# Linear attention of one layer: a list schedule in place of a hand-written round order, PSUM banks divided by use, its own weights loaded first

## The chip, the cores and the metric

The kernel runs on one core of a Trainium2 chip. The core has five engines that run side by side and wait for one another through semaphores: PE (TensorE, the matmuls; PEld is its weight load), DVE (VectorE), ACT (ScalarE), POOL (GpSimd) and SP (SyncE, which here only issues DMAs). Each engine executes its own instructions strictly in the order in which they stand in its queue. SBUF is the working memory of 128 partitions. PSUM, which the matmuls write, has eight banks of 2 KB a partition; a tile of 128 x 512 float32 fills one.

The metric is the device time of one execution in microseconds (us). The kernel before took 3962.16 us, the median of three runs (3951.46, 3962.16, 3969.95).

## The reference

The program is four layers of a network over x of shape 4 x 32 x 128 x 128 (batch, t, n, feature), all float32: graph attention with a state-space scan, a Fourier-domain attention, **linear attention and a mixture of experts (layer 2)**, a second softmax attention and a recurrent layer. The change is within the first half of layer 2, cut here to what it computes (`bs` 4, `seq` 4096, 8 heads of 16):

```python
def _ln_t(v, eps=1e-5):
    m = jnp.mean(v, axis=-1, keepdims=True)
    s = jnp.var(v, axis=-1, keepdims=True)
    return (v - m) / jnp.sqrt(s + eps)

def _L2_attn_ref(Q, Wq, bq, Wk, bk, Wv, bv, Wo, bo):
    q = (Q @ Wq + bq).reshape(bs, seq, N_HEADS, HEAD_DIM)
    k = (Q @ Wk + bk).reshape(bs, seq, N_HEADS, HEAD_DIM)
    v = (Q @ Wv + bv).reshape(bs, seq, N_HEADS, HEAD_DIM)
    phi_q = jax.nn.elu(q) + 1.0
    phi_k = jax.nn.elu(k) + 1.0
    KV = jnp.einsum('blhd,blhm->bhdm', phi_k, v)
    K_sum = phi_k.sum(axis=1)
    Z = 1.0 / (jnp.einsum('blhd,bhd->blh', phi_q, K_sum) + EPS)
    V_new = jnp.einsum('blhd,bhdm->blhm', phi_q, KV) * Z[..., None]
    return V_new.reshape(bs, seq, N_HEADS * HEAD_DIM) @ Wo + bo

t = t + _L2_attn_ref(_ln_t(t), ...)          # layer 2, first half
t = t + _L2_ffn_ref(_ln_t(t), ...)           # layer 2, experts
```

All keys of a batch element must be summed into KV before its first query can be answered.

## The kernel before

The activations stay in SBUF for the whole program, in the tile X: 128 images of 128 x 128, 32 for each batch element. Layer 2's attention (`linear_attention`, L2001) works on groups of four images, 128 x 512 numbers; there are 32 groups u, eight for each batch element. Each group passes two halves.

The **first half** makes the keys. *stats* (DVE, L2033, L2035, and L250 for the added epsilon) and *power* (POOL, L251, one over the root) give the layer norm's factors. *norm* (DVE, L2042, four instructions) writes xn. *turn* (PE, L257, four transposes into a PSUM bank "pt") and a copy by ACT (L2051, called *turned* below) give ln, the transposed group, which is kept in one of 12 buffers until its queries. *keys* (PE, L2056) multiplies ln by Wk and Wv side by side into the two banks "pk". *keys_out* is four instructions: ACT copies the values (L2063, *vout*), DVE adds the key bias (L2064, *kadd*), ACT makes a relu and an exponential (L2066, L2067, *krelu* and *kexp*). *keys_elu* (DVE, L2071, *kelu*) finishes phi(k), and *gather* (PE, L2078) adds the group to KV in the bank "pKV". After eight groups *gathered* (DVE, L2088 to L2091) takes KV out.

The **second half** answers the queries: *queries* (PE, L2095, into a bank "pt"), *queries_out* (ACT, L2100, L2101, L2102: two relus that read the bank, and an exponential; *qout* and *qexp* below), *queries_elu* (POOL, L2105, *qelu*), *attend* (PE, L2111, into the two banks "pn"), *attended* (DVE, L2117 to L2119), *back* (PE, L257, transposes into "pt") with a copy by ACT (L2129, *backed*), *project* (PE, L2135, into "pt"), and *add* (DVE, L2141), which adds the result to X. *bias* (POOL, L2138) adds bo to X and may run any time after the group's norm.

The order on each engine is written out by hand. A loop of 46 rounds (L2150) calls every step once, each for a group that lies a fixed number of rounds back; queries come ten rounds after stats. `in_order` ties each engine's instructions to just that order:

```python
            for r in range(U + 14):
                do(norm, r - 1)
                do(keys, r - 2)
                do(queries, r - 10)
                ...
                do(project, r - 13)
                do(stats, r)
                do(add, r - 13)
                ...
```

PSUM is divided so: three banks "pt", which turn, queries, back and project take in turn; two "pk"; two "pn"; one "pKV". `layer2` (L2175) first asks SP for the first eight loads of the experts' weights, 1 MB each (`expert_load`, L2194), and then calls `layer2a`, whose first lines ask SP for the attention's own nine small weights (L200 and L2008). The route, the experts and the scatter of layer 2 follow it.

Other stages of the same program, the graph attention of layer 0 (L384 on) and the attention of layer 3 (L2563), already use a planner, `Parts` (L124). A stage adds its parts to it, each with its engine, an assumed cost in us, the parts that it comes after, the buffers that it takes and frees ("holds" with a limit), and a rank. `emit` (L166) then builds the program part by part: among the first `window` parts left it looks for those whose inputs and buffers are settled, finds the earliest possible start by the assumed costs, and among the parts of that engine that could start within `patience` of it takes the one of lowest rank. So the order on each engine is fixed when the program is built; at run time the engines follow it and wait where a semaphore is late.

Of the kernel before, what the change touches and what calls it, by code (L numbers as in the profile page):

```python
# [19 lines left out]
P = 128  # L20
# [167 lines left out]
class Kernel:  # L188
# [1807 lines left out]
    def layer2a(self):  # L1996
        with self.pool("l2c", 1) as c, self.pool("l2w", 2) as w:
            with self.pool("l2pt", 3, True) as pt, self.pool("l2pk", 1, True) as pk, self.pool("l2pv", 1, True) as pv:
                self.linear_attention(c, w, pt, pk, pv)

    def linear_attention(self, c, w, pt, pk, pv):  # L2001
# [10 lines left out]
        vs = [c.tile([P, 4, P + 1], F32, tag=f"v{i}", name=f"v{i}") for i in range(2)]  # L2012
# [6 lines left out]
        def bank():  # L2019
            return pt.tile([P, 4, P], F32, tag="pt", name="pt")  # L2020
# [7 lines left out]
        def stats(u):  # L2028
            st = w.tile([P, 4, 6], F32, tag="st", name="st")
            mv = S[u]["mv"] = w.tile([P, 4, 2], F32, tag="mv", name="mv")  # L2030
            rs = S[u]["rs"] = w.tile([P, 4], F32, tag="rs", name="rs")
            for i in range(4):
                nc.vector.bn_stats(st[:, i, :], xs(u)[:, i, :])  # L2033
            for i in range(4):
                nc.vector.bn_aggr(mv[:, i, :], st[:, i, :])  # L2035
            self.rsqrt(rs, mv[:, :, 1], 1e-5)
# [9 lines left out]
        def turn(u):  # L2046
            p = bank()
            x = S[u].pop("xn")
            self.transposes(p, [x[:, i, :] for i in range(4)])
            S[u]["ln"] = w.tile([P, 512], F32, tag="ln", name="ln", bufs=12)  # L2050
            nc.scalar.copy(S[u]["ln"], flat(p))  # L2051
# [6 lines left out]
        def keys_out(u):  # L2058

            p = S[u].pop("kv")  # L2060
            k = S[u]["k"] = w.tile([P, 4, P], F32, tag="k", name="k")
            m = S[u]["m"] = w.tile([P, 4, P], F32, tag="m", name="m")
            nc.scalar.copy(vs[u % 2][:, :, :P], p[:, :, 1, :])  # L2063
            nc.vector.tensor_tensor(k, p[:, :, 0, :], bk.unsqueeze(1).to_broadcast([P, 4, P]), ALU.add)  # L2064

            nc.scalar.activation(m, k, AF.Relu, scale=-1.0)  # L2066
            nc.scalar.activation(m, m, AF.Exp, scale=-1.0)  # L2067
# [5 lines left out]
        def gather(u):  # L2073
            if u % 8 == 0:
                KV["p"] = pv.tile([P, P + 1], F32, tag="pKV", name="pKV")
            k = S[u].pop("k")
            for i in range(4):
                nc.tensor.matmul(  # L2078
                    KV["p"], k[:, i, :], vs[u % 2][:, i, :], start=(u % 8 == 0 and i == 0), stop=(u % 8 == 7 and i == 3)
                )  # L2080

        def gathered(u):

            if u % 8 == 7:
                p = KV.pop("p")
                t = KV[u // 8] = w.tile([P, P + 8], F32, tag="KV", name="KV")
                ks = w.tile([P, 1], F32, tag="ks", name="ks")
                nc.vector.tensor_copy(ks, p[:, P : P + 1])  # L2088
                nc.vector.scalar_tensor_tensor(t[:, :P], bv, ks, p[:, :P], ALU.mult, ALU.add)
                nc.vector.tensor_tensor(t[:, :P], t[:, :P], m16, ALU.mult)  # L2090
                nc.vector.tensor_scalar(t[:, P:], m16[:, 0:P:16], ks, None, ALU.mult)  # L2091

        def queries(u):
            S[u]["pq"] = bank()
            nc.tensor.matmul(flat(S[u]["pq"]), Wq, S[u].pop("ln"), start=True, stop=True)  # L2095

        def queries_out(u):
            q = S[u]["q"] = w.tile([P, 512], F32, tag="q", name="q")
            m = S[u]["m"] = w.tile([P, 512], F32, tag="mq", name="mq")
            nc.scalar.activation(m, flat(S[u]["pq"]), AF.Relu, scale=-1.0, bias=nbq)  # L2100
            nc.scalar.activation(q, flat(S[u].pop("pq")), AF.Relu, bias=bq)  # L2101
            nc.scalar.activation(m, m, AF.Exp, scale=-1.0)  # L2102

        def queries_elu(u):
            nc.gpsimd.tensor_tensor(S[u]["q"], S[u]["q"], S[u].pop("m"), ALU.add)  # L2105
# [18 lines left out]
        def back(u):  # L2124
            p = bank()
            z = S[u].pop("z").rearrange("p a h d -> p a (h d)")
            self.transposes(p, [z[:, i, :] for i in range(4)])
            S[u]["zT"] = w.tile([P, 4, P], F32, tag="zT", name="zT")
            nc.scalar.copy(S[u]["zT"], p)  # L2129

        def project(u):
            p = S[u]["po"] = bank()
# [10 lines left out]
        def do(f, u):  # L2143
            if 0 <= u < U:
                f(u)

        nbq = c.tile([P, 1], F32, tag="nbq", name="nbq")
        nc.vector.tensor_scalar(nbq, bq, -1.0, None, ALU.mult)
# [866 lines left out]
```

## Time and profile before

| what | value |
|---|---|
| three runs | 3951.46, 3962.16, 3969.95 us |
| profiled execution, its own time | 3967.12 us |
| span of the profiled execution | 3965.3 us |
| mean granted PE clock | 0.888 of full speed |
| busy PE / DVE / ACT / POOL over the span | 81% / 78% / 66% / 61% |
| linear attention: first stats (L2033) to end of last add (L2141) | 2959.0 to 3252.6 us |
| first keys (L2056); keys of group 2; keys of group 9 | 2975.6; 2990.8; 3030.1 us |
| last gather (L2078) | 3221.1 us |

The profile is of one execution; it is some 5 us slower than the median of the three runs. A row of a timeline or a group gives the start or the sum, the duration, the engine, the line, the operation, the tiles out<-in, the shapes and the count; in square brackets or behind the bar stands the idle time of the engine just before, and what ended it. DVE's 78% over the whole program says little of one stage; this case is read from the 294 us of the linear attention.

### The profile page before, as it was taken

What the parts mean: (1) busy time and instruction counts of PE and PEld (TensorE: products, weight loads), DVE (VectorE), ACT (ScalarE), POOL (GpSimd) and SP (SyncE); (2) the same over time, 40 slices, a digit from 0 to 9 for tenths busy, and PEclk for the clock granted to TensorE, in tenths of its full rate; (3) what the DMA queues carried; (4) which work ended last, traced back from release to release, by engine and by line L of the source; (5) the groups of instructions that cost most, each with busy time, mean ns of one, the idle gap of its engine ahead of it and who ended that gap; (6) DMA issues with size and microseconds to landing.
All of it is one profiled execution on the core that took longest, in us unless ns stands there. A gap on an engine that the chain in (4) does not pass through costs nothing. (4 is left out here: it accounts for less than half of the span.)

```text
span 3965.3 us, 64167 instructions
## 1 busy us (share of the span) xinstructions
PE 3227.2 (81%) x23297; PEld 2075.9 (52%) x23297; DVE 3090.5 (78%) x7595; ACT 2609.6 (66%) x5093; POOL 2400.4 (61%) x1786
## 2 busy tenths in 40 slices
PE   6888887888888888878888869787847787988877
PEld 3445544444544454544444548655535663587655
DVE  6799997799997799997899975668757866286952
ACT  5799875798864798865899853334544556166763
POOL 2599883699873699973799860233444443066940
PEclk8999889999888999998999885888769998998999
DMA  3000000000000000000000000000020000600003
GB/s 122 1 1 1 1 1 1 1 1 1 1 1 1 1 1 1 1 1 1 1 1 1 1 17 2 1 1 1 1 87 8 1 1 1 256 7 1 1 1 86
DMA packets 51548, 61.34 MB, mean 15 GB/s; under 512 B 5743, under 2 KB 31036, under 8 KB 51100
## 3 DMA queue, kind: packets, MB, share of 16 engines
q1 hardware_dynamic: 36636, 42.12, 3.1%
q10 hardware_dynamic: 14592, 15.08, 1.1%
q8 instruction: 187, 3.06, 0.3%
q14 instruction: 133, 1.09, 0.1%
HBM read 48.79 MB, written 8.39 MB: 14 GB/s over the span
## 5 line engine op out<-in xcount | busy, mean ns | idle before, releaser
L667 POOL TENSOR_TENSOR e<-dt,Ar 128x1024 f32<-128x1024 f32 x496 | 1160.9, 2362 | 103.4 <-ACT pa L673 101.0
L695 DVE SCALAR_TENSOR_TENSOR S<-u,BC,pa 128x256 f32<-128x256 f32 x1984 | 820.8, 476 | 28.4 <-PE yp L710 0.5
L687 DVE TENSOR_TENSOR pa<-pa,S 128x1024 f32<-128x1024 f32 x496 | 607.3, 1224 | 49.3 <-ACT pa L673 49.0
L673 ACT ACTIVATE pa<-e 128x1024 f32<-128x1024 f32 x496 | 504.8, 1023 | 126.8 <-DVE S L695 114.4
L710 PE MATMUL yp<-S,D 64*64 64x256 f32 x4096 | 378.4, 414 | 101.7 <-DVE S L695 87.3
L710 PE MATMUL yp<-S,Dp 64*64 64x256 f32 x4096 | 342.9, 452 | 51.2 <-DVE S L695 38.4
L710 PEld LDWEIGHTS yp<-S,D 64*64 64x64 f32 x4096 | 186.4, 140 | 264.4 <-DVE S L695 153.8
L465 POOL TENSOR_TENSOR e<-e,den 128x512 f32<-128x512 f32 x128 | 132.2, 1043 | 257.2 <-DVE den L461 193.2
L710 PEld LDWEIGHTS yp<-S,Dp 64*64 64x64 f32 x4096 | 175.7, 153 | 203.5 <-issue 118.1
L679 ACT ACTIVATE D<-I,BC 128x64 f32<-128x64 f32 x1024 | 260.7, 334 | 0.6 <-PE yp L710 0.6
L889 PE MATMUL pm<-h,Wm 128*128 128x512 f32 x512 | 240.1, 604 | 1.2 <-ACT h L525 1.2
L728 PE MATMUL pm<-I,y 128*128 128x64 f32 x1024 | 165.1, 289 | 89.7 <-ACT y L718 89.7
L453 ACT ACTIVATE e<-sc,mn 128x128 f32<-128x128 f32 x512 | 143.9, 391 | 98.1 <-DVE mn L448 96.6
L728 PEld LDWEIGHTS pm<-I,y 128*128 128x128 f32 x1024 | 152.4, 214 | 101.9 <-ACT y L718 101.9
L673 ACT ACT_TABLE_LOAD x144 | 184.8, 1283 | 19.4 <-DVE S L695 17.2
L684 POOL TENSOR_TENSOR Dp<-I,BC 128x256 f32<-128x256 f32 x256 | 164.4, 660 | 20.1 <-PE yp L710 10.4
L251 POOL TENSOR_TENSOR rs<-rs,mhalf 128x4 f32<-128x4 f32 (+1 forms) x33 | 38.6, 1171 | 220.0 <-DVE rs L250 181.7
L448 DVE TENSOR_REDUCE mn<-sc 128x4 f32<-128x512 f32 x128 | 83.4, 685 | 87.8 <-PE sc L440 55.9
L889 PEld LDWEIGHTS pm<-h,Wm 128*128 128x128 f32 x512 | 90.9, 191 | 92.3 <-issue 90.2
L723 PE MATMUL pm<-xc,DD 128*128 128x128 f32 x512 | 127.8, 334 | 5.3 <-ACT sz L859 4.6
L723 PEld LDWEIGHTS pm<-xc,DD 128*128 128x128 f32 x512 | 87.6, 210 | 64.9 <-issue 38.0
L2607 ACT ACTIVATE xn<-X,xnb,xrs 128x128 f32<-128x128 f32 x192 | 80.7, 488 | 42.6 <-DMA lnw<-in_L_attn_ln_w_dram 30.3
(587 smaller groups left out, 8025.7 us busy)
## 6 DMA issues: line engine op xcount, KB each, us to landing
w<-in_L_ffn_weight_dram SPq DMA_DIRECT2D x22, 1024.0 KB
w<-in_L_ffn_weight_dram ACTq DMA_DIRECT2D x10, 1024.0 KB
out_dram<-o ACTq DMA_DIRECT2D x16, 256.0 KB
out_dram<-o SPq DMA_DIRECT2D x16, 256.0 KB
X<-in_x_dram SPq DMA_DIRECT2D x4, 512.0 KB
A<-in_L_conv_A_log_dram SPq DMA_DIRECT2D x1, 2048.0 KB
cw<-in_L_conv_conv_w_dram SPq DMA_DIRECT2D x1, 512.0 KB
sh<-in_sh_dram SPq DMA_DIRECT2D x1, 512.0 KB
```

The lines of the kernel that those rows point to most:

```text
L453: nc.scalar.activation(e[:, i, :], v["sc"][:, h, i * P : (i + 1) * P], AF.Exp, scale=-1.0, bias=v["mn"][:, 4 * h + i : 4 * h + i + 1],)
L465: nc.gpsimd.tensor_tensor(v["e", h], v["e", h], den, ALU.mult)
L667: nc.gpsimd.tensor_tensor(v["e", q], node("dt").unsqueeze(1).to_broadcast([P, 4, 256]), Ar[:, 4 * q : 4 * q + 4, :], ALU.mult)
L673: nc.scalar.activation(v["a", q], v.pop(("e", q)), AF.Exp, scale=-1.0)
L679: nc.scalar.activation(v["D", q][:, r, :], I2, AF.Copy, scale=g["BC"][:, i, s : s + 1])
L684: nc.gpsimd.tensor_tensor(v["D", q], I2.unsqueeze(1).to_broadcast([P, 4, 64]), C, ALU.mult)
L687: nc.vector.tensor_tensor(v["a", q], v["a", q], S[:, 4 * q : 4 * q + 4, :], ALU.mult)
L695: nc.vector.scalar_tensor_tensor(S[:, s, :], node("u"), Bt, a[:, r, :], ALU.mult, ALU.add)
L710: nc.tensor.matmul(v["y"][o : o + 64, n, :256], D[ns, r, :], S[ns, s, :], start=(s < 2), stop=(s >= 14), skip_group_check=True,)
L723: nc.tensor.matmul(v["p"][:, j * P : (j + 1) * P], DD[:, j, :], g["xc"][:, j, cs], start=True, stop=False)
L728: nc.tensor.matmul(v["p"][:, o : o + 64], v["y"][:, n, j * P : (j + 1) * P], I2, start=False, stop=(n == 1))
L889: nc.tensor.matmul(g["x", j], Wm[:, i, j * P : (j + 1) * P], rows(4 * k + 3 - i), start=(i == 0), stop=(i == 3))
```

## The change

The loop of rounds is gone. Every step becomes one or more parts of a planner (`window` 300, `patience` 0.3), all 32 groups in one plan, and the order on each engine is what the planner makes of it. For that, steps are cut finer: the rsqrt into a DVE part and a POOL part (power), turn and back into a PE part and an ACT copy (turned, backed), keys_out into vout, kadd, krelu and kexp, queries_out into qout and qexp. The second half of group u enters the plan behind the first half of group u + 8; the ranks are `at` x 125.5 plus a number by kind.

The PSUM banks are divided by use: "pt" has two banks, for turn and back; a new bank "pq" is for queries and project; "pk", "pn" and "pKV" stay as they were. stats' small tiles have three buffers in place of two, and there are three value tiles v in place of two (one more memset of its column of ones). Instructions and shapes are otherwise the same.

The eight expert loads are asked for after the attention's own nine loads, by the `loads()` that `layer2` passes in.

In the order that the planner makes, nbq stands first on DVE, then stats0, stats1, norm0, norm1, stats2, stats3, kadd0; PE begins turn0, keys0, turn1, queries0, keys1, turn2, turn3, gather0, keys2. From the middle of the plan PE reads "keys21 back10 queries12 attend11 turn22 gather20 back11 keys22 project9 attend12 queries13 turn23 back12 project10 keys23 attend13 queries14 gather21 back13 project11 turn24 queries15 keys24 project12 attend14 queries16 gather22 back14 project13 attend15 queries17 turn25 back15 project14 keys25"; DVE "kadd21 stats26 kelu21 attended11 norm24 stats27 kadd22 add9 attended12 kelu22 norm25 stats28 add10 attended13 kadd23 add11 kelu23 norm26 stats29 add12 attended14 kadd24 add13 kelu24 attended15"; POOL takes bias some two groups after its norm. After gather31 eight attends, six queries and ten projects are left.

```diff
-    def layer2a(self):
+    def layer2a(self, loads):
         with self.pool("l2c", 1) as c, self.pool("l2w", 2) as w:
-            with self.pool("l2pt", 3, True) as pt, self.pool("l2pk", 1, True) as pk, self.pool("l2pv", 1, True) as pv:
-                self.linear_attention(c, w, pt, pk, pv)
+            with self.pool("l2pt", 2, True) as pt, self.pool("l2pk", 1, True) as pk:
+                self.linear_attention(c, w, pt, pk, loads)
...
+    L2_RANKS = dict(
+        add=432.5, attend=163, attended=143.5, back=-446, backed=241, bias=0, gather=334.5, gathered=-397,
+        kadd=81.5, kelu=-133.5, kexp=135, keys=-316.5, krelu=358, norm=-14.5, power=152.5, project=194.5,
+        qelu=303, qexp=546.5, qout=333, queries=-184, stats=-112, turn=79.5, turned=-372, vout=-17.5,
+    )
...
-        vs = [c.tile([P, 4, P + 1], F32, tag=f"v{i}", name=f"v{i}") for i in range(2)]
+        loads()
+        vs = [c.tile([P, 4, P + 1], F32, tag=f"v{i}", name=f"v{i}") for i in range(3)]
...
+        plan = Parts(window=300, patience=0.3)
+        hold, pace = plan.hold, 125.5
+        def part(kind, at, *args, **kwargs):
+            plan.rank = at * pace + self.L2_RANKS[kind]
+            return plan.add(*args, **kwargs)
...
         def queries(u):
-            S[u]["pq"] = bank()
+            S[u]["pq"] = bank(pk, "pq")
...
         def project(u):
-            p = S[u]["po"] = bank()
+            p = S[u]["po"] = bank(pk, "pq")
...
+        def first(u, at):
+            hs, hx, hp, hl = hold("st", 3), hold("xn", 2), hold("pt", 2), hold("ln", 12)
+            p = part("stats", at, DVE, 1.95, lambda: stats(u), (), [hs])
+            p = part("power", at, POOL, 1.0, lambda: power(u), [p])
+            p = part("norm", at, DVE, 1.5, lambda: norm(u), [p], [hx], [hs])
+            p = part("turn", at, PE, 0.8, lambda: turn(u), [p], [hp], [hx])
+            S[u]["turned"] = p = part("turned", at, ACT, 0.6, lambda: turned(u), [p], [hl], [hp])
+            hp, hv, hk, hm = hold("pk", 1), hold("v", 3), hold("k", 2), hold("m", 2)
+            p = part("keys", at, PE, 2.0, lambda: keys(u), [p], [hp], [hl])
+            v = part("vout", at, ACT, 0.6, lambda: values_out(u), [p], [hv], [hp])
+            k = part("kadd", at, DVE, 0.7, lambda: keys_add(u), [p], [hk], [hp])
+            m = part("krelu", at, ACT, 0.63, lambda: keys_relu(u), [k], [hm])
+            m = part("kexp", at, ACT, 0.63, lambda: keys_exp(u), [m], table="exp")
+            k = part("kelu", at, DVE, 0.7, lambda: keys_elu(u), [m], (), [hm])
+            last = part("gather", at, PE, 1.1, lambda: gather(u), [v, k, last], () if u % 8 else [hg], [hv, hk])
...
+        def second(u, at, ready):
+            hp, hq, hn, hz = hold("pq", 1), hold("q", 2), hold("pn", 1), hold("z", 2)
+            p = part("queries", at, PE, 1.0, lambda: queries(u), [S[u]["turned"]], [hp], [S[u]["hl"]])
+            p = part("qout", at, ACT, 1.26, lambda: queries_out(u), [p], [hq], [hp])
+            p = part("qexp", at, ACT, 0.63, lambda: queries_exp(u), [p], table="exp")
+            p = part("qelu", at, POOL, 1.06, lambda: queries_elu(u), [p])
+            p = part("attend", at, PE, 1.2, lambda: attend(u), [p, ready], [hn], [hq, S[u]["hK"]])
+            p = part("attended", at, DVE, 1.15, lambda: attended(u), [p], [hz], [hn])
+            hp, hT, ho = hold("pt", 2), hold("zT", 2), hold("pq", 1)
+            p = part("back", at, PE, 0.8, lambda: back(u), [p], [hp], [hz])
+            p = part("backed", at, ACT, 0.6, lambda: backed(u), [p], [hT], [hp])
+            p = part("project", at, PE, 1.1, lambda: project(u), [p], [ho], [hT])
+            b = part("bias", at, POOL, 1.27, lambda: bias(u), [S[u]["normed"]])
+            part("add", at, DVE, 0.7, lambda: add(u), [p, b], (), [ho])
+        for r in range(U + 8):
+            if r < U:
+                first(r, r)
+            if r >= 8:
+                second(r - 8, r + 1, ready[(r - 8) // 8])
         with self.in_order():
-            for r in range(U + 14):
-                do(norm, r - 1)
...
-                do(bias, r - 3)
+            plan.emit()
...
     def layer2(self):
         with self.pool("l2A", 1) as pa:
             bufs = {}
-            for q in range(self.NA):
-                self.expert_load(pa, bufs, q)
-            self.layer2a()
+            self.layer2a(lambda: [self.expert_load(pa, bufs, q) for q in range(self.NA)])
```

## The prediction

> **What bounds the kernel now.** I read the page first, then the DMA issues (to place the stage), then the stretches, groups and timeline inside it. The change touches one stage alone, the linear attention of layer 2: from the first L2033 at 2959.0 us to the last L2141, which ends at 3252.6, 293.6 us of a span of 3965.3. Nothing of another stage changes its instructions.
>
> The stretches of this stage of the kernel before (columns: stretch, length, busy us of PE, PEld, DVE, ACT, POOL, each with its count, then clock, DMA share, GB/s):
> ```profile
> 2959.00:2975.60 16.60, 1.16 (x4) 0.75 (x5) 4.78 (x26) 0.59 (x1) 2.03 (x2) 0.50 1.02 383
> 2975.60:2990.80 15.20, 10.27 (x32) 8.17 (x32) 6.19 (x27) 5.92 (x9) 1.44 (x2) 0.66 0.11 29
> 2990.80:3030.10 39.30, 28.36 (x142) 20.57 (x142) 32.06 (x106) 16.30 (x29) 19.27 (x15) 1.00 0.00 1
> 3061.20:3216.60 155.40, 123.66 (x809) 105.91 (x810) 126.61 (x357) 86.14 (x154) 73.81 (x56) 1.00 0.00 1
> 3216.60:3250.00 33.40, 30.87 (x215) 24.72 (x214) 19.03 (x42) 20.39 (x36) 13.90 (x11) 1.00 0.00 1
> ```
> They are: waiting for weights; two rounds at a low PE clock; seven fill rounds of 5.6 us (keys2 at 2990.8 to keys9 at 3030.1); 19 steady rounds of 8.18; the tail. In the steady rounds DVE is busy for 126.6/19 = 6.66 us a round and PE for 6.51, so neither is full. The timeline and the groups of the steady stretch say why:
> ```profile
> 2966.94 0.60 SPq L2008 DMA_DIRECT2D Wkv<-in_L_attn_Wk_dram  x1
> 2975.61 3.75 PE L2056 MATMUL pk<-Wkv,ln 128*128 128x256 f32 x8 [12.36 <-DMA Wkv<-in_L_attn_Wv_dram]
> 2976.75 0.15 DVE L2148 TENSOR_SCALAR nbq<-bq 128x1 f32<-128x1 f32 x1 [10.53 <-DMA bq<-in_L_attn_bq_dram]
> ...
> 3103.30 1.16 PE L2135 MATMUL pt<-Wo,zT 128*128 128x128 f32 x8 [1.97 <-ACT q L2101]
> 3104.50 0.69 DVE L2141 TENSOR_TENSOR X<-X,pt 128x512 f32<-128x512 f32 x1 [1.25 <-PE pt L2135]
> ```
> ```profile
> L2042 DVE TENSOR_SCALAR xn<-X,mv,rs 128x128 f32<-128x128 f32 x72 | 35.1, 546 | 0.0
> L2071 DVE SCALAR_TENSOR_TENSOR k<-k,m 128x512 f32<-128x512 f32 x19 | 22.1, 1165 | 0.0
> L2141 DVE TENSOR_TENSOR X<-X,pt 128x512 f32<-128x512 f32 x20 | 13.8, 688 | 23.1 <-PE pt L2135 23.1
> L2135 PE MATMUL pt<-Wo,zT 128*128 128x128 f32 x160 | 23.1, 287 | 32.6 <-ACT q L2101 32.6
> ```
> The first keys (L2056) wait 12.4 us for weights queued behind the experts'. Each steady round has one ring: the project matmuls (L2135) wait for the PSUM bank that ACT frees with L2101 (32.6 us over the stretch), and DVE's residual add (L2141), next in DVE's fixed order, waits for project (23.1 us). Those are nearly all of DVE's 28.8 idle us.
>
> **The change, part by part.** The arithmetic is the same: the same matmuls, ACT operations and vector operations; one more memset of 128x4 on POOL (two took 0.14 us).
>
> *Weights first.* SP's first load of the stage still waits for DVE's L1973 and is issued at 2950.85; now the nine small loads stand there. Their issues took 0.33 to 0.60 us each once the queue was clear, so Wv, the fourth, is issued by about 2953 and lands about 2 us later (bq: issued 2974.70, used 2976.75). The first ln is ready at 2963.9 (ACT's L2051 starts at 2963.34 and takes 0.59), so keys0 starts at about 2964.1 in place of 2975.6. New in DVE's order: nbq stands ahead of the first stats and waits for bq, the eighth load, landing between 2956 and 2961; the stats cannot start before 2959.0 anyway (they wait for POOL's L1838), so 0 to 2 us, and I take 0. The eight expert loads (8.4 MB, 22 us at 383 GB/s) move 5 us back and land by about 2983; they are used after 3250, some 265 us of cover, cost 0. PE starts at half clock (keys 3.75 us, later 1.89; clock 0.50 and 0.66 in the first stretches) and was at full clock some 12 us after the first keys: keys0, turn1, queries0 and keys1 end to end are 3.75 + 1.06 + 2.04 + 3.75 = 10.6, turn2, turn3 and gather0 at full clock 2.3, so keys2 at 2977.0 against 2990.8: **13.8 us gained**. Bounds 8 (nbq late, half clock for longer) and 16 (full clock early).
>
> *Fill, keys2 to keys9.* Before: 5.61 us a round, DVE busy about 4.6, then 0.9 waiting for POOL's power (L251). In the new order stats run one or two groups ahead, so that wait has cover. DVE's own work: stats 0.86 + 0.36 + 0.17, norm 1.12 to 2.05, kadd 0.68, kelu 0.69 to 0.97: 3.9 to 5.1; I take 4.7, 7 x 0.9 = **6 us gained**. Bounds 2 and 11. Two of queries0 to 2 fall in here; PE has room (28.4 of 39.3).
>
> *Steady, keys9 to the last gather (gather31, 3030.1 to 3221.1 before).* 22 first halves and 24 second halves, 23 pairs: 191 us, 8.3 a pair. I bound the new pitch three ways. (1) By hand, with durations from the rows before, along the new order from keys21 to keys25 (each part starts when its engine, its inputs and its bank are free): keys start at 0, 6.7, 13.5, 21.6 and 33.3 us, while 4 first and about 5.5 second halves pass (queries12 to 17), 4.75 pairs: 7.0 a pair. It leaves out blocks of DVE by POOL. (2) By share. The same planner orders the attention of layer 3 and that of layer 0, and there the stretches read:
> ```profile
> 3500.00:3520.00 20.00, 17.37 (x102) 16.03 (x102) 17.80 (x79) 15.40 (x33) 13.61 (x15) 1.00 0.01 1
> 3520.00:3540.00 20.00, 18.98 (x112) 17.93 (x110) 15.92 (x70) 16.02 (x36) 14.93 (x18) 1.00 0.01 1
> 3540.00:3560.00 20.00, 18.17 (x122) 17.83 (x123) 17.06 (x79) 16.17 (x36) 16.17 (x19) 1.00 0.01 2
> 660.00:680.00 20.00, 16.02 (x158) 9.98 (x158) 17.94 (x47) 13.03 (x38) 7.43 (x8) 1.00 0.00 1
> ```
> Its fullest engine is at 91% (PE, 54.5 of 60) and 90% (DVE). Here DVE's 6.66 at 88% give 7.6, PE's 6.51 at 91% give 7.15. (3) Nothing gained: 8.3. I take 7.6, DVE being the fuller engine: 23 x 7.6 = 175, **16 us gained**; with 7.0 it is 30, with 8.3 nothing.
>
> *Port.* norm took 1.12 us at 2961.60 and 2.05 at 2991.91, where POOL's bias (L2138, 1.26 us) had begun 0.06 earlier; kelu 0.69 or 1.17. So some 1.3 us a pair of DVE's time is blocking by POOL, and where POOL's parts fall now is new. The Trainium skill, "SBUF — State Buffer", section "SBUF: two separate sides", says that VectorE and GpSimd share a port pair as an exclusive lock and that the loser blocks for the whole instruction; the row agrees (0.93 lost of 1.26). By that rule a worst order would leave no steady gain and about 3952; by the row's average it is the sum below.
>
> *Tail, gather31 to the last add.* Before 31.5 us. Transposes have two banks now, but queries and project share one, pq. Its ring: queries 1.02, ACT's two relus 1.26, project 1.06, add 0.69 and some 0.3 of handovers, 4.35 a round against 3.4 now. About 3 us, five rounds of 4.4 to queries31, then 10: 35, **3.5 us lost**. Bounds 0 and 9 (5.4 a round, if exp stands behind a late zT copy). In steady rounds 4.35 fits in 7.6, and so do ACT's 97 us of the 155 when spread.
>
> **Sum.** 13.8 + 6 + 16.2 - 3.5 = 32.5 us. The profiled execution took 3967.1 (span 3965.3 and 1.8 around it): 3935. It lies 5.0 above the median of 3962.2, so for a median 3930.
>
> **Rivals.** *Better packing*: the hand walk's 7.0 holds, PE bounds: 13.8 + 6 + 30 - 3.5 = 46, 3916. For it: PE reaches 91% in layer 3. Against: the walk has no blocks.
>
> *Port, no steady gain.* Each pair has two steps of DVE that can be blocked, norm and kelu. If each waits out one whole POOL operation of 1.27, DVE needs 5.85 + 2.54 = 8.4 a pair: 193 us, -2; with 2 for the fill, 13.8 + 2 - 2 - 3.5 = 10, 3952. For it: kelu is blocked in nearly every steady round now. Against: in the new order bias follows norm instead of running into it.
>
> *One bank, slower.* pq decides from the pitch at which its ring outgrows the round. Own time 4.35; if, each round, relus queue behind three ACT copies (1.8), add behind norm and stats (3.4) and project behind one PE neighbour (0.9), it is 10.45: 23 x 10.45 = 240, -49, total -33, 3995. Break-even is (191 + 16)/23 = 9.0, and slower by 0.5% from 9.9. For it: the ring is the same kind of wait that costs 32.6 us now, and each planned order rests on assumed costs (PE 8.0 a pair, measured 6.5). Against: in the new order add stands two or three parts behind its project. The Trainium skill, "Perfetto Trace Analysis", section "Optimization Strategy", says that a gap that repeats on the fullest engine can mean too little SBUF or PSUM for the next tile; the gap at L2141 is such a one, and by that rule one bank for two uses keeps it.
>
> **How the numbers follow.** 0.5% is 20 us, about what a measurement here can tell from no change (the three runs lie 18 apart). Forecast (20 to 45 gained) 0.63, better packing 0.11, port or another stall that eats the steady gain 0.17, one bank 0.09. Faster 0.74, same 0.17, slower 0.09. The range runs from steady pitch 7.0 with a 16 us start (3910, less 2) to no gain at all, 3962; it leaves out one bank and a little of either side.
>
> **What would show it.** Right: PE's first keys within 2 us of 2964; nbq's wait under 2; DVE at 88% or more in the steady stretch and L2141's successor idle for under 8 us in all; a tail of 4.4 us a round with queries waiting for the add. Wrong: keys at 8 us or more apart; norm and kelu together over 3.5 us a pair (port); queries or project waiting over 2 us a round for pq; an unchanged start, if SP's first small load waits for something later than 2950.85.

## The result, and the profile after

The changed kernel took 3922.15 us (median of four runs, 3916.93 to 3928.68) against 3966.05 us for the kernel before on the same chip (four runs, 3951.46 to 3974.04): a ratio of 0.989, 95% interval 0.9871 to 0.9909. It is faster by 1.1%. The forecast was 3930 in a range of 3908 to 3962.

The four runs of one kernel lie 12 and 23 us apart, and much of that is not of this stage: outside the linear attention, in code that no kernel here changes, the thirteen profiled executions lie 13.3 us apart (3662.9 to 3676.2). The span of the changed kernel is 50.2 us shorter (3915.1 against 3965.3), of which 3.9 lie outside the linear attention, in unchanged code. So everything below is read from the stage itself, cut at four events that both kernels have. *Start* runs from the first stats to the keys of group 2, *fill* from there to the keys of group 9, *steady* from there to the last gather, *tail* from there to the end of the last add; the last gather counts from its start. One correction to the text on record: keys of group 9 began at 3031.8 us in the kernel before, not at 3030.1, so its fill was 41.0 us (six rounds of 5.6 and one of 7.3) and its steady stretch 189.3.

| us | start | fill | steady | tail | stage |
|---|---|---|---|---|---|
| before | 31.8 | 41.0 | 189.3 | 31.5 | 293.6 |
| after | 14.7 | 31.8 | 163.0 | 37.8 | 247.3 |
| gained | 17.1 | 9.2 | 26.3 | -6.3 | 46.3 |
| forecast | 13.8 | 6 | 16.2 | -3.5 | 32.5 |

The stretches of the stage of the changed kernel (columns as in the prediction: stretch, length, busy us of PE, PEld, DVE, ACT, POOL with counts, granted PE clock, DMA share, GB/s):
```profile
2957.20:2962.20 5.00, 1.16 (x5) 0.74 (x5) 4.75 (x23) 0.59 (x1) 3.29 (x4) 0.50 1.05 408
2962.20:2972.00 9.80, 9.53 (x39) 7.49 (x40) 8.85 (x36) 5.51 (x9) 6.26 (x6) 0.74 1.05 407
2972.00:3003.80 31.80, 25.59 (x143) 20.31 (x141) 27.75 (x101) 18.64 (x34) 18.28 (x16) 1.00 0.22 78
3003.80:3166.70 162.90, 150.61 (x962) 126.52 (x963) 133.17 (x429) 105.17 (x185) 82.89 (x67) 1.00 0.00 1
3166.70:3204.50 37.80, 30.94 (x201) 24.04 (x199) 18.04 (x40) 17.54 (x30) 8.88 (x7) 1.00 0.00 0
```
The wait for weights has gone: the first stretch, 16.6 us before, is 5.0. In the steady stretch PE is busy 150.6 of 162.9 us, 92%. Its work is the same as before (151.0 us between the same two events); the time around it is what went. DVE's work did not stay the same: for almost the same operations (423 and 429) it was busy 153.5 us before and 133.2 after.

The timeline of the start, rows of three engines (the load of Wkv, nbq, the first and the second keys):
```profile
2949.94 0.43 SPq L2014 DMA_DIRECT2D Wkv<-in_L_attn_Wk_dram  x1
2956.89 0.15 DVE L2174 TENSOR_SCALAR nbq<-bq 128x1 f32<-128x1 f32 x1 [6.83 <-DMA bq<-in_L_attn_bq_dram]
2962.19 3.78 PE L2076 MATMUL pk<-Wkv,ln 128*128 128x256 f32 x8 [0.73 <-ACT ln L2071]
2967.79 1.89 PE L2076 MATMUL pk<-Wkv,ln 128*128 128x256 f32 x8
```
The keys wait 0.73 us for ln and no longer 12.36 for a weight. nbq waits for its load, but ends before the first stats at 2957.24. The second keys already take 1.89 us, at full clock.

The groups of the steady stretch that answer to the four shown before (L2060 is norm, L2097 kelu, L2171 add, L2165 project):
```profile
L2165 PE MATMUL pq<-Wo,zT 128*128 128x128 f32 x176 | 24.1, 280 | 2.7 <-ACT q L2127 2.5
L2060 DVE TENSOR_SCALAR xn<-X,mv,rs 128x128 f32<-128x128 f32 x88 | 32.4, 430 | 0.0
L2097 DVE SCALAR_TENSOR_TENSOR k<-k,m 128x512 f32<-128x512 f32 x24 | 16.6, 691 | 4.2 <-ACT m L2093 3.6
L2171 DVE TENSOR_TENSOR X<-X,pq 128x512 f32<-128x512 f32 x22 | 14.9, 680 | 5.4 <-PE pq L2165 5.4
```
Project's wait for ACT is 2.5 us in place of 32.6, the add's wait for project 5.4 in place of 23.1. A piece of norm has 430 ns (546 in the rows of the prediction, 598 over the whole steady stretch of before), kelu 691 (1165 and 1081).

The steady stretch by 40 us:
```profile
3000.00:3040.00 40.00, 36.84 (x241) 31.66 (x240) 38.73 (x133) 26.05 (x48) 24.14 (x20) 1.00 0.01 1
3040.00:3080.00 40.00, 36.33 (x233) 30.46 (x232) 38.13 (x136) 25.50 (x45) 24.85 (x20) 1.00 0.00 1
3080.00:3120.00 40.00, 36.21 (x228) 29.68 (x227) 32.55 (x107) 24.45 (x44) 20.92 (x17) 1.00 0.01 1
3120.00:3160.00 40.00, 37.93 (x249) 32.23 (x249) 23.38 (x60) 26.93 (x48) 13.55 (x11) 1.00 0.00 1
```
PE is at 91 to 95% throughout. DVE is at 97 and 95% in the first 80 us and at 58% in the last 40: the planned order takes DVE's heavier first halves early and leaves second halves, which are PE's, for later (the last stats end at 3124 us). A mean share of 82% hides that DVE has nothing to spare in the first half.

### The profile page after: what moved, and what is told of

It reads as the page before. It is cut to its first block, busy times and chain, and to the rows that moved or that the text cites. A ratio compares the mean times of both kernels' runs of the same rounds, so it can differ in the third digit from the quotient of the medians.

```text
span 3915.1 us, 64166 instructions
## 1 busy us (share of the span) xinstructions
PE 3214.2 (82%) x23297; PEld 2068.5 (53%) x23297; DVE 3067.3 (78%) x7595; ACT 2608.9 (67%) x5093; POOL 2394.2 (61%) x1787
## 5 line engine op out<-in xcount | busy, mean ns | idle before, releaser
L723 PEld LDWEIGHTS pm<-xc,DD 128*128 128x128 f32 x512 | 86.2, 207 | 65.0 <-issue 40.1
L2663 ACT ACTIVATE xn<-X,xnb,xrs 128x128 f32<-128x128 f32 x192 | 80.7, 487 | 42.4 <-DMA lnw<-in_L_attn_ln_w_dram 30.2
L1726 POOL TENSOR_TENSOR n<-n,mhalf 16x1 f32<-16x1 f32 x40 | 21.5, 537 | 138.9 <-DVE n L1866 40.9
```

The source lines that it names most:

```text
L723: nc.tensor.matmul(v["p"][:, j * P : (j + 1) * P], DD[:, j, :], g["xc"][:, j, cs], start=True, stop=False)
```

## The experiments

All stage lengths, cut as above, from one profiled execution of each kernel. The ratios are to the kernel before on the same chip; where none stands, the kernel ran once.

| kernel | whole, us | ratio (95%) | start | fill | steady | tail | stage |
|---|---|---|---|---|---|---|---|
| before, own loads first | 3960.15 | 0.9987 (0.9967 to 1.0007) | 20.1 | 41.0 | 197.9 | 31.5 | 290.5 |
| before, bias ahead of stats | 3962.61 | 0.9979 (0.9964 to 0.9994) | 31.8 | 41.0 | 182.5 | 31.5 | 286.8 |
| before, both of these | 3937.84 | | 20.1 | 38.0 | 180.7 | 31.5 | 270.3 |
| before, without POOL's bias and qelu | 3953.71 | | 31.7 | 40.8 | 176.1 | 29.5 | 278.2 |
| before, banks divided | 3975.37 | 1.002 (1.0002 to 1.0037) | 31.9 | 41.0 | 194.0 | 40.1 | 306.9 |
| after, experts' loads first | 3937.09 | 0.9922 (0.9905 to 0.9938) | 26.4 | 31.8 | 163.0 | 37.8 | 259.0 |
| after, banks shared | 3922.43 | 0.9882 (0.9863 to 0.99) | 14.7 | 31.9 | 168.8 | 30.2 | 245.7 |
| after, bias behind a later power | 3919.01 | 0.9899 (0.9863 to 0.9935) | 14.5 | 30.2 | 169.5 | 37.9 | 252.1 |
| after, ranks by kind at zero | 3944.65 | | 14.7 | 36.7 | 169.9 | 52.0 | 273.3 |
| after, late projects in pk | 3920.47 | 0.9888 (0.9852 to 0.9924) | 14.7 | 31.8 | 163.0 | 35.5 | 245.0 |
| after, that and the tail's order tied | 3914.2 | 0.9864 (0.9844 to 0.9884) | 14.7 | 31.8 | 163.9 | 30.8 | 241.2 |

**The loads alone, in both orders.** The first kernel takes the kernel before and moves only the experts' loads; the second takes the changed kernel and moves them back.

```diff
-            for q in range(self.NA):
-                self.expert_load(pa, bufs, q)
-            self.layer2a()
+            self.layer2a(lambda: [self.expert_load(pa, bufs, q) for q in range(self.NA)])
```


> The kernel before with one part of the change alone: the attention's own nine loads asked for ahead of the experts' eight. Theory A (the start gain is the weights' and passes through to the end, since the rounds follow one another without slack): keys0 within 1 us of 5.0 us after the first stats, keys2 some 14 to 17 us earlier against the first stats, the stage (first stats to end of last add, 293.6 us before) 277 to 280, the total 14 to 17 us shorter. Rival B (the start was also shortened by the new order, which interleaves the first groups): keys2 only 11 to 12 us earlier, stage 282.

```diff
-            self.layer2a(lambda: [self.expert_load(pa, bufs, q) for q in range(self.NA)])
+            for q in range(self.NA):
+                self.expert_load(pa, bufs, q)
+            self.layer2a(lambda: None)
```


> The changed kernel with the experts' loads ahead again. Theory A: keys0 12 us later against the first stats, all of it kept to the end: stage 247.3 plus 11 to 14, about 260, total 3933 to 3936. Rival (the planner's order has slack to take the late start up, as stats and norms run ahead): under 6 us longer, 3925 to 3928.

Both give the same number: the start is 11.7 us longer with the experts' loads in front (31.8 against 20.1 in the hand order, 26.4 against 14.7 in the planned one), and in the planned order fill, steady and tail are unchanged to 0.1 us. So 11.7 of the start's 17.1 us are the loads, and the other 5.4 are the order: in the hand order PE stands idle for 3.62 us ahead of the second keys, waiting for ln, and these then take 3.65 us at half clock; in the planned order turn and queries follow the first keys without a gap, and the second keys take 1.89. So the start in the hand order is what the rival of the first text expected (11 to 12 us); the stage of 290.5 us is what neither expected, since the steady stretch of that execution was 8.6 us longer (the last section says why). The whole time does not settle it: 11.7 us are 0.3%, and its interval reaches from 0.33% shorter to 0.07% longer.

**POOL against DVE in the hand order.** The first edit lets POOL take bias of the group just normalised, ahead of stats, so that it starts behind norm. The second takes POOL's two large operations out altogether: that kernel leaves out bo and the exponential part of phi(q), so its time is that of a stage with less to compute.

```diff
             for r in range(U + 14):
...
+                do(bias, r - 1)
                 do(stats, r)
...
-                do(bias, r - 3)
```


> The kernel before with one call moved in its round: POOL's bias is for the group normalised just before (r - 1 in place of r - 3) and stands ahead of power and qelu, so it runs behind norm in place of alongside it. Theory P (the steady gain of the change is mostly DVE no longer blocked by POOL: norm 2.05 us alongside bias, 1.11 alone, and norm stands in the ring that sets the round): norm near 1.1 us, the round from 8.18 us to about 7.3, the stage from 293.6 to 272 to 278. Rival O (the gain is the planner's interleaving; the ring over project and the shared bank sets the round whatever DVE's load): round 7.9 to 8.2, stage 285 or more.

```diff
-                do(queries_elu, r - 10)
+                do(lambda u: S[u].pop('m'), r - 10)
...
-                do(bias, r - 3)
```


> The kernel before, in its hand-written order, with POOL's bias and qelu left out (X lacks bo, and phi(q) lacks its exponential): only power is left on POOL. Theory P, the ring ADD, kelu, norm, kadd, krelu, kexp, qout, project, back to ADD sets the round, and the blocks by POOL lie inside it: norm 1.11 and kelu 0.69 in place of 1.95 and 1.17, so the round falls by 1.3, from 8.1 to 6.7 to 6.9. Rival O: the order itself holds the round at 7.4 or more.

With bias moved, a round of the hand order fell from 8.11 us to 7.66. The groups of DVE in its steady rounds say what was exchanged:
```profile
L2071 DVE SCALAR_TENSOR_TENSOR k<-k,m 128x512 f32<-128x512 f32 x17 | 26.5, 1558 | 0.0
L2042 DVE TENSOR_SCALAR xn<-X,mv,rs 128x128 f32<-128x128 f32 x68 | 18.8, 335 | 0.0
```
norm is free of blocks (335 ns a piece), and kelu now runs into POOL's qelu and takes 1558 ns. Without POOL's two large operations norm is at 342 and kelu at 685 ns, and a round takes 7.66 us again. That round lies between what the two theories of the first kernel expected (7.3, and 7.9 to 8.2), as does its stage of 286.8 us. Something else held it there, which I had not seen: a second ring. Its links in the timeline of the kernel without POOL's bias and qelu:
```profile
3111.67 0.59 ACT L2063 COPY v<-pk 128x512 f32<-128x512 f32 x1 [2.39 <-PE pk L2056]
3112.29 0.69 DVE L2064 TENSOR_TENSOR k<-pk,bk 128x512 f32<-128x512 f32 x1 [0.92 <-ACT v L2063]
3113.02 0.63 ACT L2066 ACTIVATE m<-k 128x512 f32<-128x512 f32 x1 [0.76 <-DVE k L2064]
3115.52 1.16 PE L2135 MATMUL pt<-Wo,zT 128*128 128x128 f32 x8 [1.23 <-ACT q L2101]
3117.41 1.89 PE L2056 MATMUL pk<-Wkv,ln 128*128 128x256 f32 x8
```
keys, then ACT's vout, then DVE's kadd, which begins only when vout is done, then ACT's relu and exponential of the keys and after them, in ACT's fixed order, the relus of the queries, whose end frees the bank for project; gather and the next keys stand behind project on PE. No step of it is lengthened by a block from POOL: kadd has its 0.69 us. So the forecast of 6.7 to 6.9 us for this kernel was wrong: in the hand order the blocks cost 0.45 us a round, some 10 us in 23 rounds, and no more, because the order itself is a ring of 7.66.

**Both cheap edits in the hand order.** How much of the gain needs the planner at all?

> The kernel before with both cheap edits of its hand order: own weights first, and bias of group r-1 ahead of stats of group r. Theory (the two gains are separate, the rest belongs to the planned order): start 20.1, fill 41.0, steady 182.5, tail 31.5, stage 275, that is 18.5 us shorter than before and some 28 us longer than the changed kernel. Rival (the second ring of the hand order, or dips of the clock, take back what one of them gives): steady 189 or more, stage 282 or more. Rival (most of the gain can be had by hand): stage 260 or less.

The stage is 270.3 us, 23.3 shorter than before: 11.7 in the start, 3.0 in the fill and 8.6 in the steady stretch. The two gains add, and the fill's 3.0 came on top of the forecast (with bias moved alone, the fill had a mean clock of 0.92 and was 41.0 long as before, with two of the dips that the last section describes; here the clock was 1.00). So the stage, forecast at 275, came out shorter than by the theory and longer than the 260 of the second rival. Half of the 46.3 us could be had by two small edits to the order as it was written; the other 23.0 came with the planned order. That order also has a third buffer for stats and a third value tile, which were not tried apart.

**The banks.** One kernel divides the banks in the hand order; the other gives the planned order three shared banks back.

```diff
-            with self.pool("l2pt", 3, True) as pt, self.pool("l2pk", 1, True) as pk, ...
+            with self.pool("l2pt", 2, True) as pt, self.pool("l2pk", 1, True) as pk, ...
...
-            S[u]["pq"] = bank()
+            S[u]["pq"] = pk.tile([P, 4, P], F32, tag="pq", name="pq")
...
-            p = S[u]["po"] = bank()
+            p = S[u]["po"] = pk.tile([P, 4, P], F32, tag="pq", name="pq")
```


> The kernel before with the division of the banks alone: two banks for turn and back, one for queries and project, in the hand-written order. Theory (a bank shared by queries and project keeps the ring; the division gains nothing by itself): steady rounds 8.0 to 8.3 us, project still waiting for ACT's relu, and the tail longer, 4.4 us a round in place of 3.4: stage 293.6 plus 5 to 12. Rival (the third shared bank was the bubble): rounds under 7.7, stage under 285.

```diff
-            with self.pool("l2pt", 2, True) as pt, self.pool("l2pk", 1, True) as pk:
+            with self.pool("l2pt", 3, True) as pt, self.pool("l2pk", 1, True) as pk:
...
-            S[u]["pq"] = bank(pk, "pq")
+            S[u]["pq"] = bank()
...
-            p = S[u]["po"] = bank(pk, "pq")
+            p = S[u]["po"] = bank()
...
-            hp, hq, hn, hz = hold("pq", 1), hold("q", 2), hold("pn", 1), hold("z", 2)
-            p = part("queries", at, PE, 1.0, lambda: queries(u), [S[u]["turned"]], [hp], [S[u]["hl"]])
-            p = part("qout", at, ACT, 1.26, lambda: queries_out(u), [p], [hq], [hp])
+            hp, hq, hn, hz = hold("pt", 3), hold("q", 2), hold("pn", 1), hold("z", 2)
+            p = part("queries", at, PE, 1.0, lambda: queries(u), [S[u]["turned"], S[u]["keyed"]], [hp, hq], [S[u]["hl"]])
+            p = part("qout", at, ACT, 1.26, lambda: queries_out(u), [p], (), [hp])
...
-            hp, hT, ho = hold("pt", 2), hold("zT", 2), hold("pq", 1)
+            hp, hT, ho = hold("pt", 3), hold("zT", 2), hold("pt", 3)
```


> The changed kernel with the PSUM banks not divided by use: three banks pt for turn, queries, back and project as before the change, planned with the same costs and ranks (queries wait for their keys and for a free q buffer, or the planner runs into a deadlock). Theory (the division is not what gains; planning is): steady pitch within 0.4 of 7.1 us, tail shorter than 37.8 us by 3 to 6 since queries need not wait for add: stage 241 to 252. Rival (the division by use is needed, as shared banks tie turn and queries together): steady pitch 7.6 or more, stage 256 or more.

In the hand order the divided banks cost 13.3 us, 8.6 in the tail and 4.7 in the steady stretch; 3.4 of these 4.7 are two more dips of the clock (last section), and rounds without a dip take 8.0 and 8.2 us as before. Project still waits for ACT's relus (35.1 us over the steady stretch). In the planned order they give 5.8 in the steady stretch and take 7.6 in the tail: with shared banks the stage is 1.6 us shorter. So this part of the change earns nothing by itself. The second kernel also adds two conditions for queries (behind the keys of the group, and with a free q), so its order differs in more than banks: DVE was busy 139.7 us in its steady stretch, in place of 133.2, with norm at 495 ns a piece, so its 5.8 us there can be blocks by POOL as well as banks. The tail is taken up separately below.

**Where the planner puts POOL's parts, and what its ranks do.** In the first kernel only POOL's order differs from the changed kernel (bias of a group comes right behind power of the third group after it); PE's, DVE's and ACT's are instruction for instruction the same. In the second all numbers by kind in the ranks are zero.

```diff
+            S[u]["powered"] = p
...
-            b = part("bias", at, POOL, 1.27, lambda: bias(u), [S[u]["normed"]])
+            b = part("bias", at, POOL, 1.27, lambda: bias(u), [S[u]["normed"], S[min(u + 3, U - 1)]["powered"]])
```


> The changed kernel with POOL's order alone altered: bias of a group comes right behind the power three groups later, so that it starts about when that group's norm does, as before the change; the order on PE, DVE and ACT is the same. Theory P (less blocking is worth much): norm and kelu together rise from 2.1 us a group towards the 3.0 of before, and the steady stretch of 163 us grows by 10 to 20. Rival O (PE is the bound now at 92%, DVE has slack): under 6 us.

```diff
-            plan.rank = at * pace + self.L2_RANKS[kind]
+            plan.rank = at * pace
```


> The changed kernel with all numbers by kind in its ranks set to zero, so that the planner only prefers the older group. Theory (what gains is that each part is placed by its inputs and banks; the numbers by kind are a detail): steady 163 to 170, stage 247 to 257. Rival (the numbers by kind make the packing, the planner alone falls back to a ring): steady 180 or more, stage 265 or more.

With bias placed to run into norm, a piece of norm in the steady stretch takes 496 ns (first row of DVE's groups in that kernel) in place of 430:
```profile
L2060 DVE TENSOR_SCALAR xn<-X,mv,rs 128x128 f32<-128x128 f32 x88 | 38.3, 496 | 0.0
```
kelu takes 716 ns for 691. DVE was busy 142.1 us in place of 133.2, 8.9 more for the same operations, and the steady stretch is 6.5 us longer, the fill 1.6 shorter. The 6.5 lie between the two expectations: DVE has less to spare than the rival says, and the blocks that this edit brings back are fewer than the theory says. About three quarters of the added time came through, which fits DVE's 95 to 97% in the first 80 us of the changed kernel.

Without the ranks the stage is 273.3 us: longer by 26.0 than with them, and no better than the hand order with its two small edits. The theory that the planner packs by inputs and banks alone, and the numbers are a detail, has fallen for the stage as a whole. It held in the steady stretch (169.9, +6.9) and failed in the tail (52.0, +14.2) and in the fill (+4.9). Groups of the tail of the kernel without ranks, and of the changed kernel, 37.8 us:
```profile
L2165 PE MATMUL pq<-Wo,zT 128*128 128x128 f32 x80 | 11.2, 283 | 6.3 <-ACT q L2127 5.7 <-ACT zT L2159 0.7
L2171 DVE TENSOR_TENSOR X<-X,pq 128x512 f32<-128x512 f32 x10 | 6.8, 683 | 19.6 <-PE pq L2165 19.6
```
```profile
L2165 PE MATMUL pq<-Wo,zT 128*128 128x128 f32 x80 | 11.5, 286 | 3.6 <-ACT q L2127 2.4 <-ACT zT L2159 0.7 <-DVE X L2171 0.3
L2171 DVE TENSOR_TENSOR X<-X,pq 128x512 f32<-128x512 f32 x10 | 6.9, 685 | 5.8 <-PE pq L2165 5.8
```
Ten projects are left in both, but eight queries without ranks in place of six, and each of them needs the one bank pq as well. Four times PE's order there puts a group's queries directly ahead of another's project, which then waits some 1.4 us for the relus; DVE's adds wait 19.6 us for project in place of 5.8. What share of the 14.2 us each of the two has was not separated; a dip of the clock in the fill and one in the tail account for up to 1.7 us each.

**The tail.** The first kernel gives the late projects the pk banks, which are idle by then; the second does so from group 22 on and also ties PE's order in the tail to attend, queries, project, back.

```diff
-            p = S[u]["po"] = bank(pk, "pq")
+            p = S[u]["po"] = bank(pk, "pq") if u < 24 else pk.tile([P, 4, 2, P], F32, tag="pk", name="pk")[:, :, 0, :]
...
-            hp, hT, ho = hold("pt", 2), hold("zT", 2), hold("pq", 1)
+            hp, hT, ho = hold("pt", 2), hold("zT", 2), hold("pq", 1) if u < 24 else hold("pk", 1)
```


> The changed kernel with project of the last batch element (groups 24 to 31) writing to the banks pk, which no keys use by then, in place of pq. Theory (in the tail the ring over the one bank pq sets 4.48 us a round): the tail falls from 37.8 to 29 to 32 us, the rest stays: stage 239 to 241, total about 3915. Rival (another ring, over qexp, qelu and attend, sets the tail): under 2 us.

```diff
+            tail = u >= 26
-            ... lambda: queries(u), [S[u]["turned"]], [hp], [S[u]["hl"]])
+            ... lambda: queries(u), [S[u]["turned"]] + ([S[u - 2]["attend"]] if tail else []), [hp], [S[u]["hl"]])
-            ... lambda: attend(u), [p, ready], [hn], [hq, S[u]["hK"]])
+            ... lambda: attend(u), [p, ready] + ([S[u - 1]["back"]] if tail else []), [hn], [hq, S[u]["hK"]])
-            ... lambda: back(u), [p], [hp], [hz])
+            ... lambda: back(u), [p] + ([S[u - 1]["project"]] if tail else []), [hp], [hz])
```


> The changed kernel with project of groups 22 to 31 in the pk banks, idle by then, and, for groups from 26 on, PE's order tied to attend, queries, project, back by added predecessors. Theory (the tail is a ring over pq, and in the earlier try with pk the irregular order took the gain): a round of 3.1 to 3.4 us, tail 30 to 32.5, start, fill and steady as in the changed kernel, stage 239.5 to 242.5. Rival (the tail is bound elsewhere, by attend, attended and back over the one pn): 4 us or more a round, tail 35 or more, stage 245 or more. Whole time some 3915, which a comparison of whole times can hardly tell from the changed kernel's.

The bank alone gave 2.3 us of the 6 to 9 that I expected; the planner had answered it with an uneven order, in which projects stand 0.9 to 5.7 us apart. With the order tied as well the tail is 30.8 us, 7.0 shorter, and a round takes 3.1 us in place of 4.5. The queries in the tail of the changed kernel (with the add that the first of them waits for), and then those of the kernel with the order tied:
```profile
3188.07 0.69 DVE L2171 TENSOR_TENSOR X<-X,pq 128x512 f32<-128x512 f32 x1 [0.34 <-PE pq L2165]
3188.81 1.13 PE L2121 MATMUL pq<-ln,Wq 128*128 128x512 f32 x2 [0.34 <-DVE X L2171]
3193.29 1.13 PE L2121 MATMUL pq<-ln,Wq 128*128 128x512 f32 x2 [0.34 <-DVE X L2171]
```
```profile
3180.18 1.02 PE L2121 MATMUL pq<-ln,Wq 128*128 128x512 f32 x2
3183.30 1.02 PE L2121 MATMUL pq<-ln,Wq 128*128 128x512 f32 x2
3186.41 1.02 PE L2121 MATMUL pq<-ln,Wq 128*128 128x512 f32 x2
```
The tied order without the further bank was not tried. This version has the shortest stage of all, 241.2 us, 6.1 less than the changed kernel. Its whole time, 0.9864 (0.9844 to 0.9884) of the kernel before, lies under the changed kernel's 0.989 (0.9871 to 0.9909), but the intervals overlap: the stage shows the gain, the whole time does not settle it.

## Why the prediction was right, and where its sizes were not

The verdict, the engines and the parts of the change that act came out as forecast. The total gain of the stage did not: 46.3 us in place of 32.5. It landed on the first rival, *better packing*, whose sum was 46; that these two agree is luck, since its terms do not (a start of 13.8, a steady gain of 30 and a tail of -3.5, measured 17.1, 26.3 and -6.3). That the whole time lies only 8 us off is partly luck: the medians measured side by side lie 43.9 us apart, where I had 32, but the kernel before had moved up by 3.9 in the meantime.

*Start, 13.8 forecast, 17.1 measured, 1.1 outside the bounds.* The mechanism was right: keys0 began 1.9 us ahead of the forecast 2964.1, and the whole stage began 1.8 us earlier. nbq cost nothing, as taken. The mis-sized term is PE's warm-up: I took 3.75 us for keys1 and 12.9 from keys0 to keys2; it took 1.89, and 9.8 in all. I had read the low clock of the first two rounds as one long warm-up. The rows of the kernel before say otherwise: turn1 ran in 0.65 us (1.06 at half clock), and the half clock of keys1 came behind a new gap, which the planned order does not have:
```profile
2979.15 0.65 PE L257 MATMUL pt<-ident,xn 128*128 128x128 f32 x4
2983.84 3.78 PE L2056 MATMUL pk<-Wkv,ln 128*128 128x256 f32 x8 [4.03 <-ACT ln L2051]
```

*Fill, 6 forecast, 9.2 measured, within the bounds.* The wait for power that I priced at 0.9 a round was 6.3 us over the fill of before, and is 0.0 after. On top came less blocking: a piece of norm fell from 589 to 379 ns there, 28 pieces or 5.9 us, of which kelu (995 ns for 692) and the added epsilon (346 for 170) took back 3.4.

*Steady, 16.2 forecast, 26.3 measured; pitch 7.6 forecast, 163.0/23 = 7.09 measured.* The step that failed is "DVE being the fuller engine": DVE's 6.66 us a pair at 88%. It carried over the blocked durations of before, though the text itself prices the blocks at 1.3 a pair; without POOL's two large operations DVE needs 123.5/23 = 5.37 in the hand order. In the changed kernel it needs 133.2/23 = 5.79 a pair, and PE, with 6.55 at 92%, is the fuller engine over the stretch. It is not the only bound: in the first 80 us DVE is the fuller one, and time added to DVE came through for the most part (6.5 of 8.9 us). The share of 88% had no row either: the row of layer 0 has 90%, which gives 7.4. Of the 26.3 us gained, 1.7 are chance: the one dip of the clock in the steady stretch of before (last section). Of my three bounds PE's (7.15) and the hand walk's (7.0) lay on either side of the measured 7.09, and I had set both aside for DVE's. In the walked part itself, keys21 to keys25, 34.7 us passed for the 33.3 walked. What I said would show the step, DVE at 88% or more, was wrong (82%); the other sign, the add idle under 8 us, was right (5.4).

*Tail, -3.5 forecast, -6.3 measured, within the bounds.* The ring over pq is as priced, 4.48 a round for 4.35 to 4.4, with queries waiting for the add (0.34). The 2.8 us missed are at its ends: from gather31 to the last queries 26.6 us passed, where I had 3 and five rounds of 4.4, since the first queries came 3.5 us behind gather31 and the first round took 5.1; and 11.3 from there to the end for the 10 taken.

*The rivals.* Port without steady gain did not come: bias behind norm left norm at 430 ns and kelu at 691, the one still somewhat blocked (342 without POOL's large operations), the other not. But the mechanism is real, as the kernel with bias behind a later power shows. The Trainium skill, "SBUF — State Buffer", section "SBUF: two separate sides", which calls the shared port an exclusive lock, agrees with that: DVE was busy 8.9 us longer for the same operations, and 6.5 us were lost. That rival's 5.85 us a pair of DVE's own work is the sum of no rows shown; 5.37 were measured. One bank did not come in the steady stretch, and did in the tail (queries wait for the add); without ranks, with two more queries left, the tail was 14.2 us longer. So the mechanism was right, and in the steady stretch the order kept it away (queries waited 1.9 us for the add in all). The Trainium skill, "Perfetto Trace Analysis", section "Optimization Strategy", says that a repeated gap can mean too few buffers. In the steady rounds the gap went with no bank added (23.1 to 5.4 us at the add), so there it was the order; in the tail a further bank, with an order that used it, closed it (37.8 to 30.8). The lower end of the range, 3910 by its words, is 3914 by the terms that it names; 3910 takes in a tail that loses nothing.

*What the prediction did not see* is the second ring of the hand order, through vout, kadd and ACT's fixed order. What I called nearly all of DVE's 28.8 idle us was 23.1, four fifths; another 2.0 was kadd waiting for vout, a link of that ring. It does not enter the sum, but it fits that the planned order gained more than a hand order freed of POOL's two large operations (steady 163.0 against 176.1).

## What to carry to other kernels

When an order changes, take the durations of an engine that shares a port from their unblocked rows and count the blocks apart; a mean of blocked rows makes that engine look like the bound. A list schedule (an order that a planner makes by ranks) is only as good as its ranks: with them at zero it was no better here than the hand order with two small edits, and 19.1 of the 26.0 us lost lay in the fill and the tail, so price these apart from the steady rounds. In a round order written by hand look for the ring that closes through an engine's fixed order: removing one wait of it shows the next ring, here 0.45 us below the first.

## What was not expected of the hardware

The granted clock of PE dips for single stretches in the middle of the stage. Two stretches of 4 us of the kernel before:
```profile
3044.00:3048.00 4.00, 1.59 (x8) 1.22 (x7) 3.06 (x12) 3.24 (x6) 2.10 (x2) 0.94 0.01 2
3048.00:3052.00 4.00, 4.00 (x15) 2.84 (x14) 2.97 (x5) 1.24 (x3) 1.68 (x2) 0.63 0.02 4
```
PE was idle for 2.41 us there, up to 3046.80, and the keys behind it took 3.12 us in place of 1.89. By the clock record of the trace the half clock began 0.7 us into these keys, at 3047.51, and ended at 3050.92, behind them. Between the keys of group 2 and the end of the stage the thirteen profiled executions have 20 such dips. Each has a granted clock of 0.50 for 3.41 us, so it takes up to 1.71 us of PE's work, and the dips of one execution begin a whole number of steps of 3.41 us apart.

The steady stretch of the kernel before has one dip and that of "own loads first" six (the first begins with the keys of group 9): five more, at 1.71 each, account for the 8.6 us by which it was longer. It has two with bias moved, three with the banks divided, one with both edits (begun just ahead of its first keys) and none without POOL's bias and qelu. The fill has two in each of the kernels with bias moved alone and without POOL's bias and qelu. Planned orders are not free of them: there is one in the fill with shared banks, and without ranks one in the fill and one in the tail. In the steady stretch of all planned kernels the clock was 1.00.

In the 3.41 us just ahead of a dip PE was busy for 0.18 to 0.50 of the time, and once for 0.65. In the changed kernel no such step between the keys of group 2 and the last gather was under 0.64, as PE's idle time comes in smaller pieces there (1.49 us at most, 2.41 before). But 19 steps of the other kernels were at 0.50 or less with no dip behind them, so a low share is not the whole rule, and no run was made to test it. The order of the rounds is the same in executions with one dip and with six; where the steps fall against the rounds differs (the first one behind the start of keys of group 9 begins 2.1 us later in the kernel before, 3.4 us later with the own loads first).

The Trainium skill, "TensorE: Matmul & The Clock Gate", Part 1, says that the clock falls to half after an idle window of about 3.4 us. At the start of "own loads first" the trace agrees: a gap of 3.62 us, then keys at half clock. In the middle of the stage it goes further than the page: the gap above was 2.41 us, and no step ahead of a dip was wholly idle.
